# Mixture-of-experts stage of a two-layer hybrid model: 128-row expert blocks, results scattered to token order, residual kept in SBUF

## The chip, the cores and the metric

The kernel runs on one core of one Trainium2 chip. Times are device microseconds of one execution, median of the runs, lower is better. The core has TensorE (PE, matrix multiplication; its weight loads are listed as PEld), VectorE (DVE), ScalarE (ACT), GpSimd (POOL) and SyncE (SP, which issues DMAs), and 16 DMA engines between HBM and the on-chip memory SBUF. Matrix products land in a second on-chip memory, PSUM.

## The reference, cut to what matters

Layer 0 is a depthwise convolution followed by a selective scan (state-space model); the change does not touch it. Layer 1 is linear attention and then a mixture of experts: for each of 4096 tokens of 256 channels, two of 16 experts are chosen and their outputs summed with weights.

```python
def _L1_ffn_ref(x, gate_w, gate_b, w1, w2, w3):
    logits = jnp.einsum('bsd,de->bse', x, gate_w) + gate_b
    probs = jax.nn.softmax(logits, axis=-1)
    top_probs, top_idx = jax.lax.top_k(probs, 2)
    top_probs = top_probs / jnp.sum(top_probs, axis=-1, keepdims=True)
    dispatch = jnp.sum(jax.nn.one_hot(top_idx, n_experts, dtype=x.dtype) * top_probs[..., None], axis=-2)
    h1 = jnp.einsum('bsd,edh->bseh', x, w1)          # w1, w2: (16, 256, 512)
    h2 = jnp.einsum('bsd,edh->bseh', x, w2)
    hidden = jax.nn.silu(h1) * h2
    expert_out = jnp.einsum('bseh,eho->bseo', hidden, w3)   # w3: (16, 512, 256)
    return jnp.einsum('bseo,bse->bso', expert_out, dispatch)
# ... cut: convolution, scan, attention
t = _to_tokens(x)                                     # (4, 1024, 256), float32
t = t + _L1_attn_ref(_ln_t(t), ...)
t = t + _L1_ffn_ref(_ln_t(t), ...)
```

## The kernel before

Everything is float32. The kernel computes only the two chosen experts of each token. The 8192 (token, expert) pairs are sorted by expert into blocks of `BS` = 256 rows; each expert's last block is padded, so 2 x 4096 / 256 + 16 - 1 = 47 blocks are always enough, and the program has 47, whatever the data. A block's expert number `eid` is read into a register of SyncE, and the block's weights (1.5 MiB) are loaded from there.

First attention, for each of the four batches `b` (`td` is the residual stream in DRAM, `xd` the normalised tokens for the experts):

```python
for b in range(NB):
    tb = att.tile([P, NT, C], F32, name="tb1", bufs=2)
    nc.sync.dma_start(out=tb, in_=rows(td, b))
    # ... cut: attention; its output is added into tb
    nc.sync.dma_start(out=rows(td, b), in_=tb)
    xe = att.tile([P, NT, C], F32, name="xe", tag="xh")
    token_layernorm(sm, xe, tb, NT, "ln3")
    nc.sync.dma_start(out=rows(xd, b), in_=xe)
    # ... cut: gate, top 2, one-hot rows hots[k], weights wts[:, k, :]
```

Then routing. Each pair's place in the sorted order is `slot`; block number `bi` and place in the block `qi` follow from it. The list `src` (which token stands in which row of which block) is made by matrix products of one-hot rows, one pair of rows for each of 2 x 32 groups of 128 tokens:

```python
pm = ps_r.tile([NBLK, BS], F32, name="pm")
for k in range(2):
    for g in range(NTA):                              # NTA = 32
        ih = rt2.tile([P, NBLK], F32, name="ih")
        nc.vector.tensor_scalar(
            ih, blocks, bi[:, k, g : g + 1], token[:, g : g + 1], ALU.is_equal, ALU.mult)
        qh = rt2.tile([P, BS], F32, name="qh")
        nc.vector.tensor_scalar(qh, places, qi[:, k, g : g + 1], None, ALU.is_equal)
        nc.tensor.matmul(pm, ih, qh, start=(n == 0), stop=(n == 2 * NTA - 1))
# ... cut: pm is copied and transposed twice into src
```

Then the experts, and last the sum in token order, where each token's two result rows are gathered by `slot`:

```python
for i in range(NBLK):                                 # wp: bufs=3, ps_h: bufs=3
    e = nc.sync.value_load(eid[0:1, i : i + 1], min_val=0, max_val=NE - 1)
    # ... cut: three loads of 512 KiB into w1, w2, w3, all issued by SyncE
    for j in range(BT):                               # BT = 2
        xb = ffn.tile([P, C], F32, name="xb", bufs=6)
        nc.gpsimd.indirect_dma_start(
            xb, None, xd[:, :], bass.IndirectOffsetOnAxis(src[:, j, i : i + 1], 0))
        # ... cut: two transposes into px
    nc.scalar.copy(xT, px)
    for hk in range(HK):                              # HK = 4, CK = 2
        p12 = ps_h.tile([P, 2, BS], F32, name="p12")
        for s, w in enumerate((w1, w2)):
            for ck in range(CK):
                nc.tensor.matmul(p12[:, s, :], w[:, ck, blk(hk, P)], xT[:, ck, :], ...)
        nc.scalar.activation(s, p12[:, 0, :], AF.Silu)
        nc.vector.tensor_tensor(hT[:, hk, :], s, p12[:, 1, :], ALU.mult)
    for j in range(BT):
        for hk in range(HK):
            nc.tensor.matmul(pf, hT[:, hk, blk(j, P)], w3[:, hk, :], ...)
        nc.vector.tensor_copy(yb[:, j, :], pf)
    nc.scalar.dma_start(out=yd[i * BS : (i + 1) * BS, :]..., in_=yb)

for q in range(NTA // TPB):                           # 8 x 4 groups of 128 tokens
    nc.sync.dma_start(out=t, in_=tds[q])
    for j in range(TPB):
        for k in range(2):
            nc.gpsimd.indirect_dma_start(
                yk, None, yd[:, :], bass.IndirectOffsetOnAxis(slot[:, k, g : g + 1], 0))
            nc.vector.scalar_tensor_tensor(
                t[:, j, :], yk, wts[:, k, g : g + 1], t[:, j, :], ALU.mult, ALU.add)
    nc.sync.dma_start(out=ofs[q], in_=t)
```

The program is written with pools of rotating buffers; a scheduler orders the instructions of each engine and sets the waits.

Of the kernel before, what the change touches and what calls it, by code (L numbers as in the profile page):

```python
# [8 lines left out]
F32 = mybir.dt.float32  # L9
I32 = mybir.dt.int32  # L10
AF = mybir.ActivationFunctionType
ALU = mybir.AluOpType
AX = mybir.AxisListType
PSUM = bass.MemoryType.PSUM

P = 128
BANK = 512

BS = 256


def over_middle(ap, n):

    return ap.unsqueeze(1).to_broadcast([ap.shape[0], n, ap.shape[1]])


def over_last(ap, n):

    return ap.unsqueeze(2).to_broadcast([ap.shape[0], ap.shape[1], n])
# [3 lines left out]
def conv_ssm_attn_moe_kernel(ctx: ExitStack, tc: tile.TileContext, a: dict, out: bass.AP):  # L33
    nc = tc.nc

    x = a["x"]
    NB, HH, WW, C = x.shape
    L = HH * WW
# [4 lines left out]
    NT = L // P  # L43
    NTA = NB * NT
    CK = C // P
    DK = DN // P
    HK = HID // P
    NHALF = L // BANK
    TPB = BANK // P
    ROWS = BANK // WW  # L50
    BT = BS // P

    NBLK = 2 * NB * L // BS + NE - 1
    assert 2 * NS == P
# [2 lines left out]
    of = out.rearrange("b h w c -> (b h w) c")  # L57
# [4 lines left out]
    dram = ctx.enter_context(tc.tile_pool(name="dram", bufs=1, space=bass.MemoryType.DRAM))  # L62
    td = dram.tile([NB * L, C], F32, name="td")

    def rows(ap, b):

        return ap[b * L : (b + 1) * L, :].rearrange("(g p) c -> p g c", p=P)

    ident = const.tile([P, P], F32, name="ident")
# [56 lines left out]
    def blk(i, n=BANK):  # L126
        return slice(i * n, (i + 1) * n)
# [6 lines left out]
    with ExitStack() as l0:  # L134
# [16 lines left out]
        with nc.allow_non_contiguous_dma(reason="small, once"):  # L151
            for m in range(DK):
                nc.scalar.dma_start(
                    out=cw[:, m, :],
                    in_=a["L0_conv_conv_w"][:, :, 0, m * P : (m + 1) * P].rearrange(
                        "i j p -> p (i j)"
                    ),
# [600 lines left out]
        with tc.manual_schedule():  # L758
# [11 lines left out]
            for k in range(n_all + 4):  # L770
# [34 lines left out]
                while True:  # L805
                    best = None
                    for i, l in enumerate(lists):
                        if not l or ready[i] + l[0][0] > k:
                            continue
                        _, eng, c, _, pb, need = l[0]  # L810
# [33 lines left out]

    hots = [l1.tile([P, NTA, NE], F32, name=f"hots{k}") for k in range(2)]
    wts = l1.tile([P, 2, NTA], F32, name="wts")
    xd = dram.tile([NB * L, C], F32, name="xd")
    yd = dram.tile([NBLK * BS, C], F32, name="yd")

    with tc.tile_pool(name="wa", bufs=1) as wa, tc.tile_pool(name="att", bufs=1) as att, \  # L850
            tc.tile_pool(name="sm", bufs=2) as sm, \
# [12 lines left out]
        )  # L864

        for b in range(NB):
            tb = att.tile([P, NT, C], F32, name="tb1", bufs=2)
            nc.sync.dma_start(out=tb, in_=rows(td, b))
            xh = att.tile([P, NT, C], F32, name="xh")
            token_layernorm(sm, xh, tb, NT, "ln2")  # L870
# [101 lines left out]
            for i in range(NT):  # L972
# [6 lines left out]
                o = sm.tile([P, C], F32, name="o1")  # L979
                nc.vector.tensor_tensor(o, po, bout, ALU.add)  # L980
                nc.gpsimd.tensor_tensor(tb[:, i, :], tb[:, i, :], o, ALU.add)  # L981
            nc.sync.dma_start(out=rows(td, b), in_=tb)


            xe = att.tile([P, NT, C], F32, name="xe", tag="xh")
            token_layernorm(sm, xe, tb, NT, "ln3")
# [53 lines left out]


    eid = l1.tile([P, NBLK], I32, name="eid")
    slot = l1.tile([P, 2, NTA], I32, name="slot")
    src = l1.tile([P, BT, NBLK], I32, name="src")
    with tc.tile_pool(name="rt", bufs=1) as rt, tc.tile_pool(name="rt2", bufs=3) as rt2, \
            tc.tile_pool(name="ps_r", bufs=1, space=PSUM) as ps_r:
        def counted(n, lo, step, name):
# [9 lines left out]
        bounds = counted(nbe, 0, BS, "bounds")  # L1057
        blocks = counted(NBLK, 0, 1, "blocks")
        places = counted(BS, 0, 1, "places")
        token = rt.tile([P, NTA], F32, name="token")  # L1060
        nc.gpsimd.iota(
            token, [[P, NTA]], base=0, channel_multiplier=1, allow_small_or_imprecise_dtypes=True
        )
        before = rt.tile([P, P], F32, name="before")
        make_upper_triangular(nc, before, 1.0, diag=False)
# [48 lines left out]
        for k in range(2):  # L1114
            nc.vector.tensor_tensor(pick, hots[k], run.rearrange("p e g -> p g e"), ALU.mult)
            nc.vector.tensor_reduce(sf[:, k, :], pick, AX.X, ALU.add)
        nc.vector.tensor_copy(slot, sf)
        part = rt.tile([P, 2, NTA], I32, name="part")
        bi = rt.tile([P, 2, NTA], F32, name="bi")
# [3 lines left out]
        nc.vector.scalar_tensor_tensor(qi, bi, -float(BS), sf, ALU.mult, ALU.add)  # L1123


        pm = ps_r.tile([NBLK, BS], F32, name="pm")
        n = 0
        for k in range(2):
            for g in range(NTA):
                ih = rt2.tile([P, NBLK], F32, name="ih")  # L1130
                nc.vector.tensor_scalar(
                    ih, blocks, bi[:, k, g : g + 1], token[:, g : g + 1], ALU.is_equal, ALU.mult
                )
                qh = rt2.tile([P, BS], F32, name="qh")
                nc.vector.tensor_scalar(qh, places, qi[:, k, g : g + 1], None, ALU.is_equal)
                nc.tensor.matmul(pm, ih, qh, start=(n == 0), stop=(n == 2 * NTA - 1))  # L1136
                n += 1
        msb = rt.tile([NBLK, BS], F32, name="msb")
        nc.vector.tensor_copy(msb, pm)
        for j in range(BT):  # L1140
            pt = ps_r.tile([P, NBLK], F32, name="pt_src")
            nc.tensor.transpose(pt, msb[:, blk(j, P)], ident[:NBLK, :NBLK])
            nc.vector.tensor_copy(src[:, j, :], pt)

    with tc.tile_pool(name="wp", bufs=3) as wp, tc.tile_pool(name="ffn", bufs=2) as ffn, \
            tc.tile_pool(name="ps_x", bufs=2, space=PSUM) as ps_x, \
            tc.tile_pool(name="ps_h", bufs=3, space=PSUM) as ps_h, \  # L1150
            tc.tile_pool(name="ps_f", bufs=2, space=PSUM) as ps_f:
        for i in range(NBLK):
            e = nc.sync.value_load(eid[0:1, i : i + 1], min_val=0, max_val=NE - 1)
            w1 = wp.tile([P, CK, HID], F32, name="w1")
            nc.sync.dma_start(
                out=w1,
                in_=a["L1_ffn_w1"][bass.ds(e, 1)].rearrange("o (k p) h -> p (o k) h", p=P),
            )
            w2 = wp.tile([P, CK, HID], F32, name="w2")
            nc.sync.dma_start(  # L1160
                out=w2,
                in_=a["L1_ffn_w2"][bass.ds(e, 1)].rearrange("o (k p) h -> p (o k) h", p=P),
            )
            w3 = wp.tile([P, HK, C], F32, name="w3")
            nc.sync.dma_start(
                out=w3,
                in_=a["L1_ffn_w3"][bass.ds(e, 1)].rearrange("o (k p) c -> p (o k) c", p=P),
            )
            xT = ffn.tile([P, CK, BS], F32, name="xT")
            px = ps_x.tile([P, CK, BS], F32, name="px")  # L1170
            for j in range(BT):
                xb = ffn.tile([P, C], F32, name="xb", bufs=6)
                nc.gpsimd.indirect_dma_start(  # L1173
                    xb, None, xd[:, :], bass.IndirectOffsetOnAxis(src[:, j, i : i + 1], 0)
                )
                for ck in range(CK):
                    nc.tensor.transpose(px[:, ck, blk(j, P)], xb[:, blk(ck, P)], ident)  # L1177
            nc.scalar.copy(xT, px)  # L1178
            hT = ffn.tile([P, HK, BS], F32, name="hT")
            for hk in range(HK):  # L1180
                p12 = ps_h.tile([P, 2, BS], F32, name="p12")
                for s, w in enumerate((w1, w2)):
                    for ck in range(CK):
                        nc.tensor.matmul(  # L1184
                            p12[:, s, :], w[:, ck, blk(hk, P)], xT[:, ck, :],
                            start=(ck == 0), stop=(ck == CK - 1),
                        )
                s = ffn.tile([P, BS], F32, name="s")
                nc.scalar.activation(s, p12[:, 0, :], AF.Silu)  # L1189
                nc.vector.tensor_tensor(hT[:, hk, :], s, p12[:, 1, :], ALU.mult)  # L1190
            yb = ffn.tile([P, BT, C], F32, name="yb")
            for j in range(BT):
                pf = ps_f.tile([P, C], F32, name="pf")
                for hk in range(HK):
                    nc.tensor.matmul(  # L1195
                        pf, hT[:, hk, blk(j, P)], w3[:, hk, :],
                        start=(hk == 0), stop=(hk == HK - 1),
                    )
                nc.vector.tensor_copy(yb[:, j, :], pf)  # L1199
            nc.scalar.dma_start(  # L1200
                out=yd[i * BS : (i + 1) * BS, :].rearrange("(j p) c -> p j c", p=P), in_=yb
            )


    with tc.tile_pool(name="fin", bufs=6) as fin:
        tds, ofs = (
            ap.rearrange("(q g p) c -> q p g c", p=P, g=TPB) for ap in (td, of)
        )
        for q in range(NTA // TPB):
            t = fin.tile([P, TPB, C], F32, name="t", bufs=3)  # L1210
            nc.sync.dma_start(out=t, in_=tds[q])
            for j in range(TPB):
                g = q * TPB + j
                for k in range(2):
                    yk = fin.tile([P, C], F32, name=f"yk{k}")
                    nc.gpsimd.indirect_dma_start(  # L1216
                        yk, None, yd[:, :], bass.IndirectOffsetOnAxis(slot[:, k, g : g + 1], 0)
                    )
                    nc.vector.scalar_tensor_tensor(
                        t[:, j, :], yk, wts[:, k, g : g + 1], t[:, j, :], ALU.mult, ALU.add  # L1220
                    )
            nc.sync.dma_start(out=ofs[q], in_=t)


_INS = [
# [30 lines left out]
```

## Time and profile before

| | |
|---|---|
| time, median of 3 runs | 4024.92 us (4021.29 to 4025.06) |
| span of the profiled execution | 4026.3 us |
| TensorE, VectorE, ScalarE, GpSimd busy | 86%, 75%, 72%, 69% of the span |
| mean granted TensorE clock | 0.952 |
| moved by DMA | 283.58 MB, 70 GB/s over the span |

The stages stand one behind the other: scan up to about 3000 us, attention to about 3350, routing to 3400, experts to 3930, sum in token order to the end. Busy shares over the whole span say little about the last three, so they are read from windows of their own. Three things help to read the lines below. A group's line ends in `busy us, mean ns of one | idle time of the engine before them and what ended it`. Matrix passes overlap, so the mean duration of one is longer than the spacing from start to start, and the spacing is what counts. L numbers are lines of the kernel before: L1131 and L1135 make the one-hot rows, L1136 multiplies them, L1173 gathers the rows of a block, L1184 is the product with w1 and w2, L1195 the one with w3, L1216 the gather of the result rows. Names of a family are merged: `p` is p12, `w` is w1, w2 or w3.

### The profile page before, as it was taken

What the parts mean: (1) busy time and instruction counts of PE and PEld (TensorE: products, weight loads), DVE (VectorE), ACT (ScalarE), POOL (GpSimd) and SP (SyncE); (2) the same over time, 40 slices, a digit from 0 to 9 for tenths busy, and PEclk for the clock granted to TensorE, in tenths of its full rate; (3) what the DMA queues carried; (4) which work ended last, traced back from release to release, by engine and by line L of the source; (5) the groups of instructions that cost most, each with busy time, mean ns of one, the idle gap of its engine ahead of it and who ended that gap; (6) DMA issues with size and microseconds to landing.
All of it is one profiled execution on the core that took longest, in us unless ns stands there. A gap on an engine that the chain in (4) does not pass through costs nothing. (4 is left out here: it accounts for less than half of the span.)

```text
span 4026.3 us, 61294 instructions
## 1 busy us (share of the span) xinstructions
PE 3469.2 (86%) x21910; PEld 2746.4 (68%) x21910; DVE 3020.1 (75%) x3820; ACT 2881.3 (72%) x4754; POOL 2770.4 (69%) x1451
## 2 busy tenths in 40 slices
PE   6788989889898988989988898799968996999990
PEld 3566667777777777777777777677755654888880
DVE  2578799899899989989998998899966556222223
ACT  1689799999999999999999999999942320111110
POOL 0669789988998899899889999999940001111106
PEclk8899999999999999999999999999988887999995
DMA  1112121112222111222211122221220002556555
GB/s 27 33 46 51 41 59 51 50 52 59 54 51 57 51 51 52 59 54 51 55 49 54 53 58 54 52 55 56 62 64 32 32 21 89 191 188 192 192 150 170
DMA packets 330468, 283.58 MB, mean 70 GB/s; under 512 B 163937, under 2 KB 234337, under 8 KB 330162
## 3 DMA queue, kind: packets, MB, share of 16 engines
q1 hardware_dynamic: 301090, 245.93, 21.6%
q0 software_dynamic: 7584, 20.72, 2.0%
q10 hardware_dynamic: 21488, 13.02, 1.0%
q8 instruction: 172, 2.82, 0.3%
q14 instruction: 134, 1.10, 0.1%
HBM read 248.90 MB, written 30.15 MB: 69 GB/s over the span
## 5 line engine op out<-in xcount | busy, mean ns | idle before, releaser
L671 POOL TENSOR_TENSOR hc<-h,cb_n 128x1024 f32<-128x1024 f32 x1024 | 2407.0, 2381 | 244.7 <-DVE h L659 174.2
L634 ACT ACTIVATE bx<-dtxT,bT 128x512 f32<-128x512 f32 x2048 | 1454.6, 711 | 169.5 <-PE ps L648 151.8
L648 PE MATMUL ps<-ident,bx 128*128 128x128 f32 x8192 | 1307.1, 281 | 245.1 <-DVE h L659 196.9
L642 ACT ACTIVATE da<-dt,l_conv_a_log_sb 128x512 f32<-128x512 f32 x2048 | 1452.5, 710 | 0.2
L648 PEld LDWEIGHTS ps<-ident,bx 128*128 128x128 f32 x8192 | 934.0, 142 | 688.9 <-issue 285.1
L681 PE MATMUL y<-ident,hc 128*128 128x128 f32 x8192 | 1248.8, 275 | 64.0 <-POOL hc L671 62.8
L659 DVE TENSOR_TENSOR_SCAN h<-da,last,ps 128x512 f32<-128x512 f32 x1024 | 1225.4, 1259 | 48.0 <-ACT da L642 21.3
L659 DVE TENSOR_TENSOR_SCAN h<-da,ps 128x512 f32<-128x512 f32 x1024 | 1179.5, 1203 | 94.6 <-ACT da L642 32.0
L681 PEld LDWEIGHTS y<-ident,hc 128*128 128x128 f32 x8192 | 965.0, 143 | 94.9 <-POOL hc L671 92.0
L1173 POOL DMA_INDIRECT xb<-xd,src x94 | 89.0, 947 | 446.5 <-PE px L1177 378.8
L1184 PE MATMUL p<-xT,w 128*128 128x256 f32 x1504 | 337.0, 382 | 5.5 <-ACT xT L1178 5.5
L1184 PEld LDWEIGHTS p<-xT,w 128*128 128x128 f32 x1504 | 285.5, 191 | 49.3 <-ACT xT L1178 10.9
L1189 ACT ACTIVATE s<-p 128x256 f32<-128x256 f32 x188 | 72.0, 383 | 340.0 <-PE p L1184 326.6
L1190 DVE TENSOR_TENSOR hT<-s,p 128x256 f32<-128x256 f32 x188 | 79.1, 421 | 308.8 <-ACT s L1189 284.0
L363 PE MATMUL bg<-pad,diag 128*128 128x512 f32 x504 | 258.2, 594 | 0.0
L981 POOL TENSOR_TENSOR tb<-tb,o 128x256 f32<-128x256 f32 x32 | 22.7, 724 | 322.5 <-DVE o L980 314.7
L1195 PE MATMUL pf<-w,hT 128*128 128x256 f32 x752 | 170.0, 379 | 0.0
L1195 PEld LDWEIGHTS pf<-w,hT 128*128 128x128 f32 x752 | 142.7, 190 | 19.6
L1178 ACT COPY xT<-px 128x512 f32<-128x512 f32 x47 | 25.4, 589 | 141.7 <-PE px L1177 80.4
L1199 DVE COPY yb<-pf 128x256 f32<-128x256 f32 x94 | 39.9, 424 | 103.1 <-PE pf L1195 103.1
L1216 POOL DMA_INDIRECT yk<-yd,slot x64 | 60.8, 950 | 66.7 <-DMA t<-td 47.5
L489 POOL TENSOR_TENSOR e<-e,s 128x512 f32<-128x512 f32 x32 | 41.1, 1287 | 71.8 <-ACT s L483 71.8
(244 smaller groups left out, 2346.1 us busy)
## 6 DMA issues: line engine op xcount, KB each, us to landing
cb_n<-cd SPq DMA_DIRECT2D x512, 256.0 KB
w<-in_L_ffn_w_dram SPq DMA_DIRECT2D x141, 512.0 KB
yd<-yb ACTq DMA_DIRECT2D x47, 256.0 KB
last<-h SPq DMA_DIRECT2D x512, 1.0 KB
xt<-in_x_dram SPq DMA_DIRECT2D x8, 512.0 KB
xr<-in_x_dram SPq DMA_DIRECT2D x32, 128.0 KB
td<-xr SPq DMA_DIRECT2D x32, 128.0 KB
tb<-td SPq DMA_DIRECT2D x4, 1024.0 KB
```

The costliest lines, as they stand in the source:

```text
L363: nc.tensor.matmul(made["bg"].rearrange("p (h w) -> p h w", w=WW), diag[:, m, k, :], pads[m][:, half * ROWS + i : (half + 1) * ROWS + i, j ...
L634: nc.scalar.activation(t, made["dtxT", u][:, j, :], AF.Copy, scale=made["bT", u][:, j, n : n + 1])
L642: nc.scalar.activation(t, made["dt", u][:, m, :], AF.Exp, scale=A[:, m, n : n + 1])
L648: nc.tensor.transpose(t[:, blk(j, P)], made["bx", s, j][:, blk(m, P)], ident)
L659: nc.vector.tensor_tensor_scan(h[:, m % 2, :], made.pop(("da", s, m)), made.pop(("dbx", s, m)), 0.0 if seg == 0 else last[b][:, n, m : m + 1],
L671: nc.gpsimd.tensor_tensor(hc, h, over_middle(made["c", s], 2), ALU.mult)
L681: nc.tensor.matmul(made["y", u][j][:, blk(m, P)], made["hc", s, m // 2][:, m % 2, blk(j, P)], ident, is_transpose=True, start=n == 0 and m ...
L1173: nc.gpsimd.indirect_dma_start(xb, None, xd[:, :], bass.IndirectOffsetOnAxis(src[:, j, i : i + 1], 0))
L1184: nc.tensor.matmul(p12[:, s, :], w[:, ck, blk(hk, P)], xT[:, ck, :], start=(ck == 0), stop=(ck == CK - 1),)
L1189: nc.scalar.activation(s, p12[:, 0, :], AF.Silu)
L1190: nc.vector.tensor_tensor(hT[:, hk, :], s, p12[:, 1, :], ALU.mult)
L1195: nc.tensor.matmul(pf, hT[:, hk, blk(j, P)], w3[:, hk, :], start=(hk == 0), stop=(hk == HK - 1),)
```

## The change

Five things are done at once. Blocks have 128 rows in place of 256, so that less padding is computed: 79 blocks. The results of a block are no longer stored in block order and gathered at the end; an indirect DMA scatters them to their place in token order (row 2 x token + k of `yd`; rows of padding go to spare rows behind), and the end loads them with plain DMAs. To know the place, the one-hot product carries the pair's number in place of the token's. The one-hot rows are made for 16 groups by one instruction, in place of one group by one. The residual stream stays in SBUF (`t_all`) from attention to the end, so `td` is neither stored nor loaded again. The pools change with it: four buffers for weights in place of three, four for p12 in PSUM, and SyncE's instructions keep the order of the program (`manual_schedule`).

```diff
-BS = 256
+BS = P
...
+    t_all = l1.tile([P, NTA, C], F32, name="t_all")
     xd = dram.tile([NB * L, C], F32, name="xd")
-    yd = dram.tile([NBLK * BS, C], F32, name="yd")
+    yd = dram.tile([2 * NB * L + P, C], F32, name="yd")
...
-            tb = att.tile([P, NT, C], F32, name="tb1", bufs=2)
+            tb = t_all[:, b * NT : (b + 1) * NT, :]
             nc.sync.dma_start(out=tb, in_=rows(td, b))
...
-            nc.sync.dma_start(out=rows(td, b), in_=tb)
...
-        pm = ps_r.tile([NBLK, BS], F32, name="pm")
+        pm = ps_r.tile([P, NBLK], F32, name="pm")
+        GC = NTA // 2
...
+            for c in range(NTA // GC):
+                gs = slice(c * GC, (c + 1) * GC)
+                qh = rt2.tile([P, GC, BS], F32, name="qh", bufs=2)
+                nc.vector.tensor_tensor(
+                    qh, over_middle(places, GC), over_last(qi[:, k, gs], BS), ALU.is_equal
+                )
+                ih = rt2.tile([P, GC, NBLK], F32, name="ih", bufs=2)
+                nc.vector.tensor_tensor(
+                    ih, over_middle(blocks, GC), over_last(bi[:, k, gs], NBLK), ALU.is_equal
+                )
+                nc.vector.tensor_tensor(ih, ih, over_last(pair[:, k, gs], NBLK), ALU.mult)
+                for j in range(GC):
+                    nc.tensor.matmul(
+                        pm, qh[:, j, :], ih[:, j, :], start=(n == 0), stop=(n == 2 * NTA - 1)
+                    )
...
+        nc.vector.tensor_scalar(none, pm, 0.0, None, ALU.is_equal)
+        nc.vector.scalar_tensor_tensor(row, none, spare, pm, ALU.mult, ALU.add)
+        nc.vector.tensor_scalar(dst, row, -1.0, None, ALU.add)
+        nc.vector.tensor_scalar(both, pm, 1.0, -1.0, ALU.max, ALU.add)
+        nc.vector.tensor_single_scalar(src, both, 1, ALU.arith_shift_right)
...
-    with tc.tile_pool(name="wp", bufs=3) as wp, tc.tile_pool(name="ffn", bufs=2) as ffn, \
+    with tc.tile_pool(name="wp", bufs=4) as wp, tc.tile_pool(name="ffn", bufs=2) as ffn, \
             tc.tile_pool(name="ps_x", bufs=2, space=PSUM) as ps_x, \
-            tc.tile_pool(name="ps_h", bufs=3, space=PSUM) as ps_h, \
-            tc.tile_pool(name="ps_f", bufs=2, space=PSUM) as ps_f:
+            tc.tile_pool(name="ps_h", bufs=4, space=PSUM) as ps_h, \
+            tc.tile_pool(name="ps_f", bufs=2, space=PSUM) as ps_f, \
+            tc.manual_schedule(engines={mybir.EngineType.SP}):
...
+            xb = ffn.tile([P, C], F32, name="xb", bufs=6)
+            nc.gpsimd.indirect_dma_start(
+                xb, None, xd[:, :], bass.IndirectOffsetOnAxis(src[:, i : i + 1], 0)
+            )
...
+            for h in range(0, HK, 2):
+                p12 = ps_h.tile([P, 2, 2, BS], F32, name="p12")
+                for j in range(2):
+                    for s, w in enumerate((w1, w2)):
+                        for ck in range(CK):
+                            nc.tensor.matmul(
+                                p12[:, j, s, :], w[:, ck, blk(h + j, P)], xT[:, ck, :],
+                                start=(ck == 0), stop=(ck == CK - 1),
+                            )
+                nc.scalar.activation(s, p12[:, :, 0, :], AF.Silu)
+                nc.vector.tensor_tensor(hT[:, h : h + 2, :], s, p12[:, :, 1, :], ALU.mult)
...
+            yb = ffn.tile([P, C], F32, name="yb", bufs=4)
+            nc.vector.tensor_copy(yb, pf)
+            nc.gpsimd.indirect_dma_start(
+                yd[:, :], bass.IndirectOffsetOnAxis(dst[:, i : i + 1], 0), yb, None
+            )
...
+            y = fin.tile([P, TPB, 2, C], F32, name="y")
+            nc.sync.dma_start(out=y, in_=yds[q])
...
-                    nc.gpsimd.indirect_dma_start(
-                        yk, None, yd[:, :], bass.IndirectOffsetOnAxis(slot[:, k, g : g + 1], 0)
-                    )
                     nc.vector.scalar_tensor_tensor(
-                        t[:, j, :], yk, wts[:, k, g : g + 1], t[:, j, :], ALU.mult, ALU.add
-                    )
-            nc.sync.dma_start(out=ofs[q], in_=t)
+                        t_all[:, g, :], y[:, j, k, :], wts[:, k, g : g + 1], t_all[:, g, :],
+                        ALU.mult, ALU.add,
+                    )
+            nc.scalar.dma_start(out=ofs[q], in_=t_all[:, q * TPB : (q + 1) * TPB, :])
```

## The prediction

> **What bounds the kernel now.** I read the 40-slice table first: the scan stage fills slices 1 to 29, and the change leaves its instructions alone (on every engine their order is the same in both kernels). So only the last 1,030 us count. Next, busy time by window, from the end of attention on (columns: window, PE, PEld, DVE, ACT, POOL busy, granted clock, DMA share, GB/s):
>
> ```profile
> 3340.00:3400.00 60.00, 42.11 (x163) 18.64 (x161) 49.35 (x183) 2.18 (x3) 2.15 (x7) 0.75 0.02 6
> ...
> 3410.00:3930.00 520.00, 514.50 (x2437) 448.87 (x2436) 118.59 (x281) 96.93 (x235) 81.24 (x86) 1.00 0.59 184
> 3930.00:4026.00 96.00, 0.52 (x3) 0.12 (x1) 30.69 (x65) 0.00 (x0) 60.80 (x64) 0.52 0.56 178
> ```
>
> Three stages, three limits: routing on VectorE (49 of 60 us), experts on TensorE (514.5 of 520 us, DMA at 0.59), and a tail in which GpSimd issues 64 gathers. The chain that ended last says the same step by step (start, length, what):
>
> ```profile
> 3366.49 32.01 PE pm L1136 x128
> 3399.80 1.17 POOL xb L1173
> 3401.28 0.95 POOL xb L1173
> 3402.54 6.38 DMA xb<-xd,src
> 3409.81 9.18 PE p L1184 x32
> ...
> 3600.13 7.17 PE p L1184 x32
> 3607.31 3.45 PE pf L1195 x16
> 3610.76 6.91 PE p L1184 x32
> ...
> 3927.07 3.47 PE pf L1195 x16
> ```
>
> To see here: a 256-row block costs 11.05 us (two blocks from 3600.13 to 3622.23), and the experts run from 3409.8 to 3930.5, 520.7 us, TensorE behind TensorE. The counts by group show that one fp32 matmul is two passes (47 blocks x 16 matmuls = 752, recorded x1504):
>
> ```profile
> L1184 PE MATMUL p<-xT,w 128*128 128x256 f32 x1504 | 337.0, 382 | 5.5 <-ACT xT L1178 5.5
> L1195 PE MATMUL pf<-w,hT 128*128 128x256 f32 x752 | 170.0, 379 | 0.0
> L1135 DVE TENSOR_SCALAR qh<-places,qi 128x256 f32<-128x256 f32 x64 | 22.1, 345 | 0.0
> L1131 DVE TENSOR_SCALAR ih<-blocks,bi,token 128x47 f32<-128x47 f32 x64 | 19.2, 301 | 1.0 <-PE pm L1136 1.0
> L1100 DVE TENSOR_TENSOR done<-end,blocks 128x752 f32<-128x752 f32 x1 | 0.9, 934 | 0.0
> ```
>
> A pass of 256 columns takes 6.91/32 = 0.216 us. What does one of 128 columns take? Two spots in the timeline tell, the second with a single column, so that only the weights count:
>
> ```profile
> 156.16 0.61 PE L689 MATMUL y<-diag_d,xg 128*128 128x128 f32 x4
> 156.61 0.60 PE L648 MATMUL ps<-ident,bx 128*128 128x128 f32 x4
> ...
> 3299.68 1.95 PE L938 MATMUL pkn<-ones,ksq 128*128 128x1 f32 x16 [0.26 <-ACT nk L942]
> ```
>
> Start to start, four passes take 0.45 us: 112 ns each. Sixteen single-column passes, 1.95 us less the drain of the last (a pass reads 250 ns): about 1.7/15 = 112 ns. So halving the columns halves the pass, and the weight load just fits under it. Last, the DMA with its queue full, when three blocks' weights load at once:
>
> ```profile
> 3402.00:3418.00 16.00, 10.23 (x35) 8.04 (x36) 1.12 (x3) 3.02 (x5) 6.85 (x8) 0.62 1.03 341
> ```
>
> Full, the 16 engines move 341 GB/s of weights and gathers.
>
> [...]
>
> **The change part by part.**
>
> *Smaller blocks, TensorE.* 79 blocks; each has 16 matmuls of 128 columns (32 passes x 0.112 = 3.58 us), 4 of 256 columns (8 x 0.216 = 1.73) and 2 transposes (0.22; the timeline has 0.109 each): 5.53 us, x79 = 437 us. Before, by the same prices, 48 x 0.216 + 4 x 0.109 = 10.8, and 11.05 were measured, 2% more. With that 2%: 445 us, against 520.7. This is the fewer padded rows: 10,112 in place of 12,032.
>
> *Smaller blocks, DMA.* Every block loads 1.5 MiB of weights whatever its rows. 79 x (1.573 MB weights + 0.131 gather + 0.131 scatter) = 145 MB, before 98.6. At 341 GB/s: 425 us. So the DMA goes from 0.59 of its time to about 0.95, just below TensorE. Four weight buffers for three let it run ahead.
>
> *The scatters.* In the program each scatter waits for the previous one to land, on GpSimd, which also issues the gathers. A gather takes 6.4 us from issue to landing on the full queue (chain above), 2.4 us in the idle tail, and 4.2 us by its packets in the trace at 0.59 load. If scatters behave alike, a chain link takes about 5 us at 0.85 to 0.95 load: just below 5.6. Four yb buffers and gathers some six blocks ahead absorb single late ones.
>
> Three limits of 445, 425 and about 400 us with small buffers between them do not reach the largest exactly; I take 5.8 us a block, 457 us: 64 us saved.
>
> *Routing.* Out: 64 pairs of tensor_scalar, 64 x (345+301) ns = 41.3 us busy, from 3366 to 3398, then a copy and two transposes (1.5 us). In: four groups of one 2048-wide and two 1264-wide tensor_tensor. From the 934 ns for 752: 1.04 ns an element and some 0.15 fixed, part of it overlapped; 2.2 + 2 x 1.4 = 5.0 us a group, 20 us in all, then the last group's 32 passes (3.6 us) and five short operations (1.2). First gather at about 3366 + 20 + 4.8 = 3391 in place of 3399.8. The wider tables before it (32 bounds, 79 blocks) cost 1.6 us more. Net -7 us.
>
> *Start of the experts.* Before, 10.0 us from first gather to first matmul: two gathers, a 512-wide copy. Now one gather is needed: -4 us.
>
> *Tail.* Before, 95.8 us from the last matmul to the end. Now: the last scatters land (5 us); loads of 8.4 MB and stores of 4.2 MB at 341 GB/s are 37 us, beside 64 adds of 0.48 us = 31 us; last store and end 7.4 us as now (from 4018.9 to 4026.3). Sum 50 us: -45.
>
> *Residual kept in SBUF.* It takes out 4 MB of stores and 4 MB of loads that no step of the chain waits for, but for the first load of the tail. In attention TensorE's order stays as it was and VectorE's normalisation statistics of later batches move forward: 0, give or take 5 us.
>
> Sum: -7 -4 -64 -45 = -120 us; 4024.9 - 120 = 3905.
>
> **The rivals.** (1) The DMA becomes the bound. For it: the ceiling is only 5% above the need, and within the saturated window there are dips near 180 to 240 GB/s. With 310 GB/s held it would be 468 us, with 290 500: total 3916 to 3948. (2) The scatter chain binds. If a landing on the full queue takes the 6.4 us of the gather plus 0.3 us to resume, 79 x 6.7 = 529 us, worse than before: total about 3977. Against: a slow chain holds back TensorE, weight loads thin out, latency falls back towards 4.2, so it limits itself near 5.5. (3) TensorE stays the bound with nothing lost: 5.55 us a block, 438 us, total 3886. (4) The weight load doesn't hide in long rows of 128-column passes (at most four in a row are seen): 125 ns would add 33 us: 3938. (5) The loads of the tail wait for more than they seem, for instance for scatters piled up: +10.
>
> **Range and chances.** The experts' 440 to 500 us carry the spread, the tail +-8, the rest +-6. So 3905, eight times in ten between 3880 and 3948. Faster by over 2% means below 3944.4: only rival 2 or a bad case of 1 fails that: 0.88. Within 2%: 0.11. Slower by over 2%: 0.01.
>
> **What would show it.** Right: the p matmuls stand at 112 ns a pass and a block at 5.6 to 5.9 us; DMA share above 0.9 and near 320 GB/s through the experts; first gather about 3391; about 50 us from last matmul to end. Wrong: TensorE idle ahead of p or pf with a weight DMA as releaser (rival 1), or ahead of px with xb, or VectorE ahead of yb with the scatter (rival 2), at 6 us a block or more.

## The result and the profile after

The changed kernel takes 3925.8 us (median of 4 runs, 3923.93 to 3929.08) against 4024.99 for the kernel before it: ratio 0.9755, 95% interval 0.9738 to 0.9772. The profiled execution has a span of 3927.3 us, 99.0 less than 4026.3. The stages, read from first and last instructions in the two traces (the first p of before is put where the prediction's chain has it, at 3409.8; its first pass starts 0.2 us earlier, beside the transposes):

| stage | before, us | after, us | difference | predicted |
|---|---|---|---|---|
| up to the first one-hot instruction | 3365.9 | 3370.3 | +4.4 | +1.6 |
| first one-hot to first gather | 33.9 | 38.1 | +4.2 | -8.6 |
| first gather to first p | 10.0 | 8.3 | -1.7 | -4 |
| experts, first p to last pf | 520.7 | 470.2 | -50.5 | -64 |
| tail, last pf to end | 95.8 | 40.4 | -55.4 | -45 |
| sum | | | -99.0 | -120 |

The prediction's own routing figure, -7, is the two first rows together. Of the +4.4, 2.6 us are already there at the end of the scan, whose instructions are the same in both; a second profile of the changed kernel starts its first one-hot instruction at 3364.9, so this row is mostly variation from one execution to the next.

The windows of the three stages, with the columns of the prediction's first fence:

```profile
3371.00:3408.40 37.40, 27.89 (x128) 27.46 (x128) 20.50 (x17) 0.00 (x0) 0.01 (x1) 0.50 0.00 0
3416.70:3886.90 470.20, 460.66 (x3316) 420.77 (x3314) 99.74 (x236) 87.29 (x237) 147.50 (x151) 1.00 0.90 304
3890.00:3927.00 37.00, 0.00 (x0) 0.00 (x0) 25.69 (x64) 0.00 (x0) 0.00 (x0) 0.52 0.93 340
```

To see here: in routing (first line) TensorE, not VectorE, is now the busiest engine, and its granted clock is 0.50, half of full speed. In the tail the GpSimd column is zero, where the kernel before had 60.8 us of gathers; the DMA works at 340 GB/s on average (392 to 401 between 3900 and 3920, less at both ends), and VectorE's 64 additions (25.7 us) fit beside it. In the experts DMA moves 304 GB/s, less than the 341 that the prediction took for its ceiling. Early in the stage it moved more than that, so 341 was no ceiling:

```profile
3440.00:3460.00 20.00, 19.51 (x141) 17.88 (x142) 4.22 (x10) 3.60 (x10) 6.18 (x8) 1.00 1.06 378
```

The chain that ended last gives the tail step by step (start, length, what):

```profile
3887.63 2.41 DMA yd<-yb,dst
...
3890.10 5.47 DMA y<-yd
...
3895.79 12.78 DVE t_all L1231 x33
3908.58 11.44 DMA y<-yd
```

One last scatter, then loads and additions; the scatters have not piled up. The groups of the experts, from the page (L1203 is the product with w1 and w2, L1212 the one with w3):

```profile
L1203 PE MATMUL p<-xT,w 128*128 128x128 f32 x2528 | 307.0, 277 | 9.5 <-ACT xT L1196 9.5
L1203 PEld LDWEIGHTS p<-xT,w 128*128 128x128 f32 x2528 | 299.4, 193 | 22.6 <-ACT xT L1196 18.6
...
L1212 PEld LDWEIGHTS pf<-w,hT 128*128 128x128 f32 x632 | 107.6, 190 | 21.6 <-DVE hT L1209 12.1
```

and what the queue of SyncE (SPq) waits for before it issues the DMAs of the weights (us in total, times, longest):

```profile
SPq L1174 <- PE p L1203: 156.1, 72, 2.8
SPq L1184 <- PE px L1194: 57.2, 36, 1.6
SPq L1184 <- PE pf L1212: 45.0, 36, 1.3
```

The DMAs of the weights wait for TensorE to give buffers back, and p and pf wait for ScalarE (xT) and VectorE (hT), not for weights. So TensorE with its hand-overs (waits for what another engine has to finish first) is the bound, and a block takes 470.2/79 = 5.95 us. Where a hand-over costs time shows in a stretch of TensorE's timeline:

```profile
3649.18 3.51 PE L1203 MATMUL p<-xT,w 128*128 128x128 f32 x30
3652.53 1.03 PE L1212 MATMUL pf<-w,hT 128*128 128x256 f32 x4
...
3654.59 0.49 PE L1194 MATMUL px<-ident,xb 128*128 128x128 f32 x3
3655.32 3.84 PE L1203 MATMUL p<-xT,w 128*128 128x128 f32 x32 [0.24 <-ACT xT L1196]
3658.99 1.03 PE L1212 MATMUL pf<-w,hT 128*128 128x256 f32 x4
```

Thirty p passes take 3.51 us with the drain of the last (a single one reads at least 272 ns), 112 ns start to start, as priced; the 277 ns of the group above are the length of one pass, and the next starts before it ends. But the scheduler put transposes directly ahead of the p passes that need their result: from the start of the transposes to the first p are 0.73 us, and the transposes need 0.33 of them (three at 0.109). The row PE says little about such waits, because the modelled ends of passes cover them (0.24 us is marked here). TensorE's weight loads, row PEld, show 0.48 us before the same pass; their idle time is the better measure, and it is used below. The kernel before, in its experts, has this one:

```profile
PEld p L1184 <- ACT xT L1178: 10.9, 23, 0.5
```

The changed kernel waits more often for xT, and also for hT:

```profile
PEld p L1203 <- ACT xT L1196: 18.6, 38, 0.8
PEld pf L1212 <- DVE hT L1209: 12.1, 40, 0.5
```

### The profile page after: what moved, and what is told of

Read it like the earlier page. It is cut to its first block, busy times and chain, and to the rows that moved or that the text cites. A ratio compares the mean times of both kernels' runs of the same rounds, so it can differ in the third digit from the quotient of the medians.

```text
span 3927.3 us, 63327 instructions
## 1 busy us (share of the span) xinstructions
PE 3413.5 (87%) x22782; PEld 2737.1 (70%) x22782; DVE 2988.4 (76%) x3661; ACT 2870.6 (73%) x4756; POOL 2777.1 (71%) x1452
## 5 line engine op out<-in xcount | busy, mean ns | idle before, releaser
L1203 PE MATMUL p<-xT,w 128*128 128x128 f32 x2528 | 307.0, 277 | 9.5 <-ACT xT L1196 9.5
L1203 PEld LDWEIGHTS p<-xT,w 128*128 128x128 f32 x2528 | 299.4, 193 | 22.6 <-ACT xT L1196 18.6
L1208 ACT ACTIVATE s<-p 128x256 f32<-128x256 f32 x158 | 60.7, 384 | 312.5 <-PE p L1203 312.5
L1209 DVE TENSOR_TENSOR hT<-s,p 128x256 f32<-128x256 f32 x158 | 66.6, 422 | 281.8 <-ACT s L1208 281.8
L983 POOL TENSOR_TENSOR t_all<-t_all,o 128x256 f32<-128x256 f32 x32 | 22.7, 726 | 322.6 <-DVE o L982 315.7
L1217 POOL DMA_INDIRECT yd<-yb,dst x79 | 77.1, 976 | 210.8 <-DVE yb L1216 98.5
L1189 POOL DMA_INDIRECT xb<-xd,src x79 | 77.8, 985 | 166.6 <-PE px L1194 94.2
L1212 PE MATMUL pf<-w,hT 128*128 128x256 f32 x632 | 170.3, 392 | 0.1
L1196 ACT COPY xT<-px 128x256 f32<-128x256 f32 x79 | 25.8, 375 | 135.2 <-PE px L1194 135.2
L1212 PEld LDWEIGHTS pf<-w,hT 128*128 128x128 f32 x632 | 107.6, 190 | 21.6 <-DVE hT L1209 12.1
L1216 DVE COPY yb<-pf 128x256 f32<-128x256 f32 x79 | 33.5, 425 | 97.3 <-PE pf L1212 97.3
L488 POOL TENSOR_TENSOR e<-e,s 128x512 f32<-128x512 f32 x32 | 41.6, 1303 | 73.0 <-ACT s L482 73.0
```

The costliest lines, as they stand in the source:

```text
L1189: nc.gpsimd.indirect_dma_start(xb, None, xd[:, :], bass.IndirectOffsetOnAxis(src[:, i : i + 1], 0))
L1203: nc.tensor.matmul(p12[:, j, s, :], w[:, ck, blk(h + j, P)], xT[:, ck, :], start=(ck == 0), stop=(ck == CK - 1),)
L1209: nc.vector.tensor_tensor(hT[:, h : h + 2, :], s, p12[:, :, 1, :], ALU.mult)
L1212: nc.tensor.matmul(pf, hT[:, hk, :], w3[:, hk, :], start=(hk == 0), stop=(hk == HK - 1))
L1217: nc.gpsimd.indirect_dma_start(yd[:, :], bass.IndirectOffsetOnAxis(dst[:, i : i + 1], 0), yb, None)
```

## The experiments

My theory after the result had two parts. Routing: 79 moving columns against 128 weight columns keep TensorE's granted clock at 0.50 (of the two operands of a pass, the one that row PEld loads is called weights here, the other moving; the loads for the thirty p passes from 3661.05 on start at 3660.84). Experts: TensorE's own order of instructions loses about 0.4 us a block, and neither the DMA nor the scatters cost anything. Every ratio below is to the kernel before, timed on the same chip; stage times are from the traces.

**The changed kernel once more.** No edit.

> The changed kernel once more, as the yardstick for the kernel with the three edits on one chip. Both theories: ratio 0.974 to 0.977 to the kernel before, first one-hot to first gather 38.1 us, experts 470 to 476 us, the range of the profiles so far with this order of TensorE.

Measured: 3930.06 us, ratio 0.9753 (0.9737 to 0.9769); one-hot to gather 38.1 us, experts 477.4, tail 40.3. The experts of one program thus vary from 470 to 477 us between executions; ten blocks take 59.4 us in the first profile from block 10 on, and 60.6 to 61.0 from block 20 on in this one. TensorE's order is the same in both, but the weight loads wait for hT 63 times and 20.2 us here, in place of 40 times and 12.1 us, which is about the difference. The 470 is the low end: the three runs below that change routing alone have 475.8, 475.3 and 478.5 us. Differences of less than 8 us in this stage are not read in what follows.

**Four one-hot buffers.**

```diff
-                qh = rt2.tile([P, GC, BS], F32, name="qh", bufs=2)
+                qh = rt2.tile([P, GC, BS], F32, name="qh", bufs=4)
-                ih = rt2.tile([P, GC, NBLK], F32, name="ih", bufs=2)
+                ih = rt2.tile([P, GC, NBLK], F32, name="ih", bufs=4)
```

> The one-hot tiles qh and ih get four buffers in place of two; nothing else. Theory (the shape of the passes, 79 moving columns against 128 weight columns, keeps the TensorE clock at 0.50): the pause of 4 us in the middle of the 128 routing passes goes, but the passes stay at 213 ns and the granted clock at 0.50, so from the first one-hot instruction to the first gather 34 us in place of 38.1; total about 3922. Rival (the pauses let the clock fall): without them the clock goes to 1.00, passes 112 ns, 25 to 27 us; total about 3914.

Measured: one-hot to gather 35.0 us, ratio 0.9766 (0.9750 to 0.9782). The stage, and a part of it in which TensorE never stops (columns as above):

```profile
3367.57:3402.59 35.02, 27.88 (x128) 27.45 (x128) 20.98 (x18) 0.00 (x0) 0.00 (x0) 0.50 0.00 0
3375.00:3400.00 25.00, 24.94 (x118) 24.73 (x117) 12.63 (x8) 0.00 (x0) 0.00 (x0) 0.50 0.00 1
```

The pause is gone, and the clock is at 0.50 through 25 us of uninterrupted passes: pauses don't explain it. The pause itself was worth 3.1 us; the total, 3933.6 us where 3922 were expected, doesn't show it (the experts of its profiled execution took 475.8 us).

**Operands exchanged.** The 79-column rows become the weights, the 128-column rows move.

```diff
-                        pm, qh[:, j, :], ih[:, j, :], start=(n == 0), stop=(n == 2 * NTA - 1)
+                        pt, ih[:, j, :], qh[:, j, :], start=(n == 0), stop=(n == 2 * NTA - 1)
...
+        nc.vector.tensor_copy(msb, pt)
+        nc.tensor.transpose(pm, msb, ident[:NBLK, :NBLK])
```

> The one-hot rows change places in the product: ih (79 columns) is loaded as weights, qh (128 columns) moves; then a copy and one transpose bring the result into the same form. Two buffers as in the changed kernel. Theory (shape): moving columns no longer fewer than weight columns, the granted clock goes to 1.00 a few us after the first pass, passes 112 ns, VectorE's 20 us set the pace, and first one-hot to first gather takes 27 us in place of 38.1 (20 us, the last 32 passes 3.6, copy and transpose 1.0, short operations 1.2, slack 1); total about 3915. Rival (pauses, or simply a cold start that needs longer than this stage lasts): the clock stays at 0.50, 38 to 39 us; total about 3926.

Measured: one-hot to gather 29.1 us, ratio 0.9729 (0.9713 to 0.9745).

```profile
3375.00:3380.00 5.00, 5.00 (x37) 5.00 (x36) 4.27 (x4) 0.00 (x0) 0.00 (x0) 0.76 0.00 0
3380.00:3385.00 5.00, 2.47 (x23) 2.24 (x21) 5.00 (x4) 0.00 (x0) 0.00 (x0) 1.00 0.01 3
3385.00:3390.00 5.00, 3.67 (x23) 3.67 (x24) 4.13 (x3) 0.00 (x0) 0.00 (x0) 0.76 0.00 0
```

The clock is at full speed some 4 us after the first pass (3373.3). It is then ahead of VectorE, stops for want of one-hot rows, and drops for a while (third line); that is the 2 us more than expected. In the kernel with three edits below, whose four buffers leave pauses of 1.5 and 1.3 us in place of this one of 3.9, the clock reads 1.00 from 3380 to 3395, the passes stay at 109 ns and the stage takes 27.1 us. So a pause of 3.9 us goes with a fall from 1.00 to 0.76 and pauses of 1.5 and 1.3 with none, while the 79-column passes stood at 0.50 with a pause of 3.8 us and without one.

**Moving rows padded to 128 columns.** Weights of 128 columns as in the changed kernel; this separates "too few moving columns" from "128-column weights".

```diff
-                ih = rt2.tile([P, GC, NBLK], F32, name="ih", bufs=2)
+                ih = rt2.tile([P, GC, P], F32, name="ih", bufs=2)
...
-                        pm, qh[:, j, :], ih[:, j, :], start=(n == 0), stop=(n == 2 * NTA - 1)
+                        pw, qh[:, j, :], ih[:, j, :], start=(n == 0), stop=(n == 2 * NTA - 1)
```

> The changed kernel, with the moving one-hot rows ih padded from 79 to 128 columns (the added columns are zero and not read); weights qh of 128 columns as before. Theory (a pass whose moving columns are fewer than its weight columns keeps the clock at 0.50): with 128 against 128 the clock goes to 1.00 within 4 us of the first pass, and VectorE sets the pace with three instructions of 2.28 us a group: 27.4 us, then 3.6 for the last passes and 1.5: 32 to 34 us from first one-hot to first gather. Rival (128-column weights of one-hot rows keep it low, and the exchange of operands helped by having 79 of them): the clock stays at 0.50, 37 to 39 us.

Measured: one-hot to gather 33.5 us, ratio 0.9754 (0.9734 to 0.9773).

```profile
3380.00:3385.00 5.00, 4.20 (x36) 3.81 (x34) 5.00 (x4) 0.00 (x0) 0.00 (x0) 1.00 0.01 3
```

Full clock, although TensorE does more work: the added columns make 128 passes cheaper, not dearer (4.6 us less for the stage, in spite of 7 us more of VectorE). Three shapes agree: 79 moving against 128 weight columns stays at 0.50, 128 against 128 and 128 against 79 rise to 1.00. The kernel before had 256 moving against 47 and stood at 1.00 from 3370 to 3380; the change turned the operands round. Nothing between 79 and 128 moving columns was tried, and the traces don't show why the clock differs.

**Half of the weights.** Weights are loaded for even blocks only; odd blocks use the weights of the block before them, so half of the weight traffic is left out.

```diff
+            if i % 2 == 0:
-            e = nc.sync.value_load(eid[0:1, i : i + 1], min_val=0, max_val=NE - 1)
+                e = nc.sync.value_load(eid[0:1, i : i + 1], min_val=0, max_val=NE - 1)
... (the three loads stand under the same condition)
```

> The changed kernel, but weights are loaded for the even blocks only and odd blocks reuse them (leaves out half of the weight traffic: 145 MB becomes 84). Theory (TensorE and the waits in its own order set the pace): experts stay at 462 to 472 us, DMA at about 0.55. Rival (the DMA sets the pace, or makes the waits): experts fall to 440 to 450 us.

Measured: experts 480.2 us, ratio 0.9779 (0.9759 to 0.9799).

```profile
3414.42:3894.57 480.15, 466.02 (x3315) 420.80 (x3314) 99.79 (x236) 87.31 (x237) 147.92 (x151) 1.00 0.49 170
```

With the DMA at 0.49 the stage is no shorter; it is 8 us above the range expected. Its weight loads wait for hT 72 times, 22.6 us, near the 66 times and 21.3 us of the padded run (478.5 us). TensorE's order is not quite the same here, so the last microseconds are not explained. The rival, DMA as bound of the changed kernel, is refuted.

**No scatter.** 128-row blocks, but results stored in block order and gathered by slot at the end.

```diff
-            nc.gpsimd.indirect_dma_start(
-                yd[:, :], bass.IndirectOffsetOnAxis(dst[:, i : i + 1], 0), yb, None
-            )
+            nc.scalar.dma_start(out=yd[i * BS : (i + 1) * BS, :], in_=yb)
...
-            nc.sync.dma_start(out=y, in_=yds[q])
+                    nc.gpsimd.indirect_dma_start(
+                        yk, None, yd[:, :], bass.IndirectOffsetOnAxis(slot[:, k, g : g + 1], 0)
+                    )
```

> 128-row blocks, but the results are stored in block order by ScalarE and gathered by slot at the end, as before the change; all else as changed. Theory (in the changed kernel scatters lie beside TensorE and cost nothing): experts 464 to 474 us, tail 92 to 97, total about 3980. Rival (the chain of scatters holds the experts up): experts 445 to 458 us, total 3955 to 3970.

Measured: 3984.77 us, ratio 0.9894 (0.9878 to 0.9911); experts 474.9 us, tail 93.2.

```profile
3413.66:3888.60 474.94, 464.83 (x3315) 420.89 (x3314) 99.59 (x236) 87.11 (x237) 68.66 (x73) 1.00 0.88 301
3890.00:3981.00 91.00, 0.00 (x0) 0.00 (x0) 31.00 (x64) 0.00 (x0) 60.84 (x64) 0.51 0.46 140
```

The scatters are worth 53 us of tail (60.8 us of GpSimd are back in the second line) and cost the experts nothing that can be seen.

**Blocks of 256 rows.** The scatter, the loads at the end, the grouped one-hot rows and the residual in SBUF are kept; weights and p12 have three buffers, p12 its form and SyncE the scheduler's order, as before the change. The one-hot product has 47 weight columns and 256 moving, as before.

```diff
-BS = P
+BS = 256
...
+            for j in range(BS // P):
... (two gathers into one px, two pf, two scatters a block)
```

> 47 blocks of 256 rows again, three weight buffers and the scheduler's own order as before; scatter, plain loads at the end, grouped one-hot rows and the residual in SBUF stay as in the changed kernel. It isolates the size of the blocks. Theory (experts bound by TensorE passes, 11.05 us a block): experts 518 to 524 us, tail 40 to 42, total 3965 to 3978. Rival (two scatters and two gathers a block cost something themselves): experts 530 us or more.

Measured: 3979.66 us, ratio 0.9880 (0.9863 to 0.9896); experts 521.0 us, tail 41.6.

```profile
3414.66:3935.68 521.02, 515.52 (x2439) 449.37 (x2438) 118.64 (x281) 97.76 (x235) 174.93 (x180) 1.00 0.58 184
```

So smaller blocks, with the buffers and the order of SyncE that came with them, are worth 43 to 51 us, all in the experts, and the tail doesn't need them. What the buffers or that order do alone was not tried.

**Experts in a fixed order.** Same operations, bytes and buffers; each engine's order is written out, so that transposes and pf stand between the two halves of p.

```diff
-            tc.manual_schedule(engines={mybir.EngineType.SP}):
+            tc.manual_schedule():
...
+        for i in range(NBLK + 1):
+            weights(i)
+            up(i, 0)            # first half of p of block i
+            turn_x(i + 1)       # transposes and xT copy of block i+1
+            down(i - 1)         # pf and yb copy of block i-1
+            up(i, 2)            # second half of p of block i
+            gather(i + 6)
+            scatter(i - 1)      # (conditions at both ends cut)
```

> The experts alone are written in a fixed order on all engines: first half of p of block i, transposes of block i+1, pf of block i-1, second half of p of block i; same buffers, same operations, same bytes. Theory (TensorE bound, and the excess over 5.53 us a block is the waits of pf for hT and of p for xT, about 0.4 us a block): 5.55 to 5.65 us a block, experts 438 to 447 us in place of 470, at 325 to 330 GB/s; total about 3898. Rival 1 (the DMA with its gathers and scatters gives no more than about 311 GB/s): experts stay at 465 to 470, SyncE no longer waits for TensorE, and TensorE waits for weights; total 3921 to 3926. Rival 2 (the scatter chain, issue to landing up to 5.9 us, now binds): 455 to 470 us, with waits of VectorE's yb copy on the scatter.

Measured: 3914.89 us, ratio 0.9721 (0.9704 to 0.9737); experts 451.5 us, tail 45.3. Neither theory alone. The stage in two parts, and its waits:

```profile
3470.00:3600.00 130.00, 130.00 (x993) 125.19 (x992) 29.80 (x71) 24.79 (x72) 44.06 (x45) 1.00 0.97 331
3600.00:3850.00 250.00, 242.28 (x1808) 226.69 (x1807) 49.10 (x130) 44.42 (x129) 81.76 (x84) 1.00 0.95 315
```

```profile
DVE yb L1233 <- DMA yd<-yb,dst: 167.8, 38, 6.0
POOL yd L1237 <- DVE yb L1233: 161.3, 44, 6.4
...
PEld pf L1229 <- DVE hT L1223: 16.0, 22, 1.4
```

Up to 3600 the theory holds: TensorE without a gap, 5.52 us a block. Then VectorE's copy into yb waits for scatters to land, holds up hT behind it, and TensorE stalls. The landing of a scatter is read at the last of the 16 packets of 4 bytes that end it in the trace. By block 36 scatters are issued 21 us after their pf, four blocks late, which is all that four yb buffers allow. From block 36 to 70 a link of the chain takes 5.9 us: 4.3 from issue to landing and 1.6 from landing to the next issue. That second part is never under about 1.1 us; it shows bare when the last scatters follow each other (start, length, idle before):

```profile
3862.17 0.97 POOL L1237 DMA_INDIRECT yd<-yb,dst  x1 [2.19 <-DMA yd<-yb,dst]
3865.31 0.97 POOL L1237 DMA_INDIRECT yd<-yb,dst  x1 [2.17 <-DVE hT L1223]
3868.46 0.97 POOL L1237 DMA_INDIRECT yd<-yb,dst  x1 [2.19 <-DMA yd<-yb,dst]
```

3.15 us a link on an idle queue: 2.05 to the landing, 1.10 to the next issue. (Lines that name another releaser than the landing are inferred; hT had long been done.) This tail of late scatters is why the tail grew by 5 us.

**Three edits together**: four one-hot buffers, exchanged operands, fixed order.

> The three edits together: four one-hot buffers, swapped operands, fixed order of the experts. If each does what its theory says, routing gives 11 to 13 us and the experts 25 to 30: total about 3886. If the experts are bound by the DMA: about 3913.

Measured: 3904.53 us, ratio 0.9689 (0.9673 to 0.9705), faster than both kernels: with 0.9753 for the changed kernel that is 0.7% less, some 26 us. One-hot to gather 27.1 us, experts 452.5, tail 46.9. The 3886 was missed by the scatters, as before.

**Two targets for the scatters.** The three edits, but odd blocks scatter into a second tensor, so that a scatter waits for the one before the last. The end reads only the first tensor: the results of odd blocks are left out of the sum.

```diff
+    yo = dram.tile([2 * NB * L + P, C], F32, name="yo")
...
-                yd[:, :], bass.IndirectOffsetOnAxis(dst[:, i : i + 1], 0), ybs.pop(i), None
+                (yo if i % 2 else yd)[:, :],
+                bass.IndirectOffsetOnAxis(dst[:, i : i + 1], 0), ybs.pop(i), None
```

> The kernel with the three edits, but odd blocks scatter into a second tensor, so that a scatter waits for the one before the last; the end reads only the first tensor (its rows are set to zero during attention), so the results of odd blocks are left out of the sum. Theory (in the kernel with a fixed order the chain of scatters, 5.92 us a link, sets the pace: yb waits for landings, scatters run four blocks late): the wait of yb for landings goes, experts fall from 452 to 438 to 446 us and the tail from 46.9 to 40 to 42. Rival (the DMA at 0.96 sets the pace, and the scatters are late because of it): experts stay at 450 us or more, now with TensorE waiting for weights.

Measured: experts 438.4 us in place of 452.5, tail 40.3; ratio 0.9702 (0.9686 to 0.9718), which can't be set against the others because the zeroing delays attention by some 24 us.

```profile
3429.20:3867.61 438.41, 438.34 (x3316) 421.34 (x3316) 99.67 (x236) 82.42 (x237) 147.55 (x151) 1.00 0.95 326
```

TensorE has no gap left in 438 us, 5.55 a block, with the DMA at 326 GB/s. A scatter takes 4.8 us to land here; with the 1.1 us of the last scatters above, one chain would need 4.8 + 1.1 = 5.9 a link, an estimate. So the chain was the limit of the fixed order, not the DMA: the same bytes in less time. Against the changed kernel, TensorE's weight loads are busy as long (421.3 and 420.8 us), while their idle time fell from 470.20 - 420.77 = 49.4 us to 17.1: the stage is shorter by 31.8 us of waits, with the same work.

**Eight result buffers**, in the kernel with the three edits.

```diff
-            yb = ffn.tile([P, C], F32, name="yb", bufs=4)
+            yb = ffn.tile([P, C], F32, name="yb", bufs=8)
```

> The kernel with the three edits, with eight yb buffers in place of four. Theory (the chain of scatters sets the pace with 5.9 us a link against 5.55 us of TensorE): TensorE may run four blocks further ahead, so the experts shorten by some 8 to 12 us, but the scatters then stand further back and the tail grows by as much; sum of experts and tail 497 to 501 as with four buffers (452.5 + 46.9), total 3900 to 3908. Rival (single late scatters, which more buffers would absorb): experts 438 to 442, tail 40 to 42, total about 3885.

Measured: 3910.9 us, ratio 0.9710 (0.9693 to 0.9726); experts 459.4, tail 47.9, together 507. The rival falls: more buffers don't absorb it. The theory's sum was missed too, by 6 us or more, though the ratio is not clear of the 0.9689 with four buffers. TensorE keeps 5.5 us a block up to block 40 in place of 20, and then is slower than with four buffers. The profile offers a cause:

```profile
POOL yd L1241 <- DMA yd<-yb,dst: 136.5, 38, 5.2
...
PE px L1207 <- DMA xb<-xd,src: 15.6, 15, 3.4
```

The scatters are now up to 29 us late, five blocks, and the gathers, six blocks ahead in the same queue of GpSimd, come late with them: transposes wait 15 times for rows. That this is all of the loss was not tested.

## Why the prediction was right, and where not

The total, 3925.8, lies within 3880 to 3948, 21 us above the 3905. The bound was named rightly: TensorE. Of the signs named for it, the 112 ns came as said; a block of 5.95 us (5.6 to 5.9 said), 304 GB/s (320), the first gather at 3408.4 (3391) and a tail of 40.4 us (50) did not, the first of them narrowly. By its steps:

- **Price of a pass.** Right: 112 ns, and the weight load hides under it, 30 loads in 3.53 us (from 3660.84) beside 30 passes in 3.51 (rival 4 falls).
- **The 2% on a block.** This is the step that failed in the experts. The prediction carried the loss of before over as a share of time: 11.05 against 10.8, so 437 became 445. But the loss is waiting at hand-overs, 0.25 us a block before and 0.42 after (5.95 - 5.53): 33 us over 79 blocks in place of 8, and up to 8 more in other executions. The lines of the weight loads show what it is made of: 23 waits for xT, 10.9 us, became 38 and 18.6 us, and 40 waits for hT, 12.1 us, came new. The other 12 us of the 457, put in for three limits close together, were for a cause that was not there: with half the weights, and without scatters, the stage is as long. That they brought the estimate nearer to 470 was luck. Rival 3 (438 us) is what TensorE takes once order and chain are out of its way: 438.4 measured.
- **DMA, 425 us at 341 GB/s.** The size of the traffic is right, and the DMA is not the bound (rival 1 falls). But 341 was the mean of one start-up window and no ceiling: the changed kernel holds 378 GB/s for 20 us and 392 to 401 in the middle of its tail. So it isn't shown that the DMA is as close behind TensorE as the 425 us say. The rate in the experts is what TensorE asks for, 304 GB/s, so "near 320 GB/s" at a share above 0.9 was a poor sign of anything: the share is 0.90 here, and 0.95 with TensorE never waiting in the run with two targets.
- **Scatter chain, about 5 us a link, just below 5.6.** Right for the changed kernel: 3.9 us (median) to land and at least 1.1 to the next issue, under 5.95. The prediction put the resume at 0.3 us in rival 2; it is 1.1. That rival became real once TensorE was faster: at 5.52 us a block the chain is the bound.
- **Routing, 20 us of VectorE and 3.6 for the last passes.** Wrong in the second term. VectorE's instructions take what was said: 2.28 and 1.47 us, 2.20 and 1.39 from start to start (3371.64, 3373.84, 3375.23). The 1.04 ns an element and 0.15 us fixed are those of a straight line through two tensor_tensor in the trace of before, 286 ns for 128 (L1019) and 934 for 752 (L1100). But the passes took 213 ns, not 112: 38.1 us is 5.1 for the first one-hot rows, 13.9 for 64 passes, a pause of 3.8, 13.9 for 64 more, and 1.4 to the gather. The prediction priced these passes as if the clock were up, as it was before with 256 moving columns, and said nothing of the operands, which the change turned round. With 128 moving columns the clock was at 1.00 some 4 to 6 us after the first pass (exchanged and padded run); with 79 it was still at 0.50 after 25 us without a pause, and the 213 ns a pass agree with that. So in these runs passes that follow each other were not enough. The slow passes also made the pause: with two buffers VectorE waits for them (2.11 and 3.15 us ahead of qh), and then TensorE for VectorE (3.77 us). By the run with four buffers it is worth 3.1 us.
- **Start, -4.** Half of it came, -1.7.
- **Tail, 50 us.** 40.4: from the last pf until the last scatter has landed and the loads start are 3.2 us, with the queue empty by then, not 5, and the 7.4 us for last store and end were counted on top of 37 us of transfers that hold the stores already. From 3890.1 to the end is 37.2 us, at 340 GB/s on average as priced, though not at an even rate; rival 5 falls.
- **Residual in SBUF, 0 give or take 5.** The traces agree: the end of attention moved by +2.8 us, of which 2.6 are carried over from the scan. It wasn't tried by itself.

The misses above the estimate (experts 13.5; routing and start about 18, of which 2.8 is variation between executions) were partly made up by the tail (10), whose price was too high. To that extent the total came out by luck.

## What to carry to other kernels

Price what engines lose at a hand-over per block, not as a share of time, and read it from the idle time of the weight loads, since the modelled ends of the passes cover it (in the changed kernel 49.4 us in row PEld, 470.20 - 460.66 = 9.5 in row PE); where a scheduler sets a producer directly ahead of its user, an order with other work between them can give it back (here, with the scatters on two chains, the stage became 31.8 us shorter). In a product like the one of routing, try the operand with fewer columns as the weights and look at the granted clock: with 79 and 128 columns that alone was worth 9 us of 38. A chain of dependent indirect DMAs had a period of landing time plus 1.1 to 1.6 us here, and the landing took from 2.05 us on an idle queue to 4.8 at a DMA share of 0.95: compare it with the new, faster block and not with the old one.

## What the runs showed of the hardware that I had not expected

- 128 fp32 passes with 79 moving and 128 weight columns held the granted clock at 0.50 for as long as they lasted (27.9 us busy, 25 us of it without a pause); padding the moving side with useless columns to 128 made the stage shorter, 33.5 us for 38.1.
- From the landing of an indirect DMA to the issue of the next one that waits for it, GpSimd took about 1.1 us at the least. Landing itself took 2.05 us on an idle queue, 2.1 (median; 2.6 on average) at a DMA share of 0.49, 3.9 to 4.4 (medians) at 0.88 to 0.94 and 4.8 at 0.95 with two chains.
- The same program's experts stage took 470 us in one execution and 477 in another, with the same clock and the same order of TensorE; the weight loads waited for hT 12.1 us in the one and 20.2 in the other. What sets this was not looked into.
